# A DFT over 121 points folded in four 64x64 tiles, paired bn_stats, and two casts exchanged between VectorE and ScalarE

## The chip, the cores and the metric

The kernel runs on one core of a Trainium2 chip. The metric is the device time of one execution in microseconds (us). The engines are TensorE (PE, its weight loads shown as PEld), VectorE (DVE), ScalarE (ACT) and GpSimd (POOL); SyncE (SP) issues most DMAs. Each engine works through its own instructions in order and waits on semaphores for the others.

## The reference

The input is 64 images of 55 x 55 pixels with 96 channels. A depthwise convolution comes first, then one block of attention-like mixing by a Fourier transform over the 3025 pixels of each image, then a quantised feed-forward network (FFN).

```python
x = lat * x + bias + x                      # lat: depthwise convolution of x
t = x.reshape(64, 3025, 96)
n = layernorm(t)
h = relu(bn1(n @ w1.T))                     # 192 hidden channels
X = fft(h, axis=1, norm='ortho')            # over the 3025 tokens
xr = relu(X.real * rd - X.imag * idg + rb)
xi = relu(X.imag * rd + X.real * idg + ib)
y = ifft(xr + 1j * xi, axis=1, norm='ortho').real
t = t + bn2(y @ w2.T)
q = lambda v: float_quantize(v, 5, 2)       # fp8, 5 exponent bits
a = lambda v: float_quantize(v, 5, 10)      # fp16
u = relu(a(a(q(layernorm(t)) @ q(W1).T) + q(b1)))   # 384 hidden channels
t = t + a(a(q(u) @ q(W2).T) + q(b2))
```

Everything but the quantised FFN is in float32.

## The kernel before

The kernel has two stages. The first is the convolution over all images; its result goes to device memory (`t1s`). The second takes the 64 images one after the other as *sequences* of 3025 = 25 x 121 tokens, and the change lies wholly in it.

The transform of 3025 points is split into 121 x 25. Token n is written as 25 j + r, with j from 0 to 120 and r from 0 to 24. A tile `t` holds j on 121 partitions and r and the channels along the free dimension. The work of one sequence runs like this:

1. `load` fetches t. `stats` (L350) makes one `bn_stats` for each of the 25 values of r, 96 channels at a time, on DVE; the instruction returns count, mean and sum of squared deviations of the even and of the odd elements, six numbers. `variance` joins the two halves with small POOL instructions (L298 to L306, with the mean where it is needed later). `root` (ACT), `inverse` (DVE) and `newton` (POOL) make the reciprocal standard deviation.
2. In seven tiles i, of four values of r each (the last has one): `scale` (L363, POOL) makes xa; `turn` (L376, PE) transposes it into PSUM (pa); `turned` (L381, ACT) copies it to tnt, 96 channels and a row of ones on the partitions, 121 columns for each r.
3. For pairs of r: `hidden` (L397, PE) multiplies tnt with the 192 columns of w1e into ph, one matmul for each r, on 121 output partitions. `relu` (L406, ACT) makes h. `dft_j` (L412, PE) multiplies h with the constant f1, 121 rows by 128 columns: cosines and sines of the needed 61 frequencies, in a padded order. Since the input is real, only these are kept. `keep` (L416, ACT) copies the result pf to g. `put` (L432) sends g to a buffer `gd` in device memory with two DMAs, of 64 partitions each.
4. `fetch` (L451) reads it back with r on the partitions; `dft_r` (L478, PE, px) does the transform over r with 64x64 tiles; three ACT instructions (L495) and four DVE instructions (L504) apply the two relus of the frequency domain, POOL joins them (L511, sm and sr). `project` (L553, L563, PE, pd), `inverse_k1` (L583, pe) and their copies on ACT (L572, L592) go back, through device memory (`put_e`, L623), to `inverse_k2` (L644, py) and the `residual` (L655, DVE), which adds to t.
5. A second layer norm with `stats` (L661), `centre` (L677) and `quantise` (L686) on POOL, transposes (L695, pq) and their copies (L700). Then the FFN in nine pieces of 1008 or 1009 columns: `up` (L718, PE, pu), `cast` (L727) from PSUM to f16 on DVE (y16), `bias` with relu (L730) on DVE (z16), `quantised` (L742) from f16 to fp8 on ACT (hq); then `down` (L762, pw), a cast (L771, ACT), a bias (L776, DVE), the residual `add` (L782, POOL) and the `store` (L788).

Every such step is a *task* with an engine, an estimated cost, a list of tasks that it comes after, and the buffers that it makes and uses. `PLACES` gives each of a sequence's tasks a due place, in units of a sequence; tasks of up to five sequences are in flight. The function `ordered` walks through all 64 sequences with these costs before anything is issued, and the order that it finds is the order of instructions on each engine. It also knows the shape of the PE tiles (`edges`), and charges 0.09 for a change of shape (`SWITCH`). The first tasks of the first two sequences (`AHEAD`, `NAHEAD`) are issued under the convolution's end.

PSUM is held by two pools in this stage: `psn`, four buffers of 512 columns, for pa, ph, pf, pd, pe, py, pq and pw; and `psw`, two buffers of 1024 columns, for px and pu. A pool hands its buffers out in turn: the fifth request waits until the first buffer's last reader is done.

Of the kernel before, what the change touches and what calls it, by code (L numbers as in the profile page):

```python
# [11 lines left out]
F32 = mybir.dt.float32  # L12
# [34 lines left out]
NR1, NJ = 25, 121  # L47
KH, KHP = 31, 32
KC = 8
UPT = 1008  # L50

AHEAD, NAHEAD = 2, 10
# [5 lines left out]
    -0.85, -0.814, -0.754, -0.694, -0.634, -0.574, -0.232, -0.28, -0.28, -0.28, -0.26146, -0.13246,  # L58
    -0.13246, 0, 0, 0.074, 0.05, 0.06623, 0.06623, 0.14023, 0.11623, 0.15385, -0.129, 0, 0, 0.13246,
    0.13246, 0.20646, 0.18246, 0.19869, 0.19869, 0.27269, 0.24869, 0.30769, 0.00346, 0.13246, 0.13246,  # L60
    0.26492, 0.26492, 0.33892, 0.31492, 0.33115, 0.33115, 0.40515, 0.38115, 0.46154, 0.13592, 0.26492,
    0.26492, 0.39738, 0.39738, 0.47138, 0.44738, 0.46361, 0.46361, 0.53761, 0.51362, 0.61538, 0.26838,
    0.39738, 0.39738, 0.52985, 0.52985, 0.60385, 0.57985, 0.59608, 0.59608, 0.67008, 0.64608, 0.76923,
    0.40085, 0.52985, 0.52985, 0.66231, 0.66231, 0.73631, 0.71231, 0.72854, 0.72854, 0.80254, 0.77854,
    0.92308, 0.53331, 0.66231, 0.66231, 0.79477, 0.79477, 0.86877, 0.84477, 1.07692, 0.72, 0.97, 1.22, 1.47,
    0.9, 0.9, 0.9, 0.9, 0.9, 0.9, 0.9, 0.9, 0.774, 0.774, 1.046, 1.046, 1.046, 1.046, 1.046, 1.046, 1.046,
    1.046, 0.92, 0.92, 1.192, 1.192, 1.192, 1.192, 1.192, 1.192, 1.192, 1.192, 1.066, 1.066, 1.514, 1.534,
    1.534, 1.584, 1.584, 1.584, 1.66, 1.68, 1.68, 1.73, 1.73, 1.73, 1.73333, 1.338, 1.338, 1.338, 1.338,
    1.338, 1.338, 1.338, 1.338, 1.212, 1.212, 1.484, 1.484, 1.484, 1.484, 1.484, 1.484, 1.484, 1.484, 1.358,
    1.358, 1.63, 1.63, 1.63, 1.63, 1.63, 1.63, 1.63, 1.63, 1.504, 1.504, 1.952, 1.972, 1.972, 2.022, 2.022,  # L70
    2.022, 2.098, 2.118, 2.118, 2.168, 2.168, 2.168, 2.23333, 2.477, 2.677, 2.677, 2.687, 2.743, 2.743,
    2.753, 2.809, 2.809, 2.819, 2.875, 2.875, 2.885, 2.941, 2.941, 2.951, 2.975, 2.927, 2.927, 2.927, 2.835,
    2.835, 3.235, 3.235, 2.856, 2.856, 3.256, 3.256, 2.877, 2.877, 3.277, 3.277, 2.898, 2.898, 3.298, 3.298,
    2.919, 2.919, 3.319, 3.319, 2.94, 2.94, 3.34, 3.34, 2.961, 2.961, 3.361, 3.361, 3.509, 3.54, 3.509,
    3.509, 3.59436, 3.62536, 3.59436, 3.59436, 3.67972, 3.71072, 3.67972, 3.67972, 3.78836, 3.81936,
    3.78836, 3.78836, 3.87372, 3.90472, 3.87372, 3.87372, 3.95908, 3.99008, 3.95908, 3.95908, 4.06772,
    4.09872, 4.06772, 4.06772, 4.15308, 4.18408, 4.15308, 4.15308, 4.23844, 4.26944, 4.23844, 4.23844,
    3.466, 3.466, 3.466, 3.266, 3.516, 3.74536, 3.74536, 3.74536, 3.54536, 3.79536, 3.83848, 3.83848,
    3.83848, 3.63848, 3.88848, 4.02472, 4.02472, 4.02472, 3.82472, 4.07472, 4.10232, 4.10232, 4.10232,
    3.90232, 4.15232,  # L80
# [4 lines left out]
def conv_attn_hybrid(ctx, tc, a, out, t1s, tb, gds, eds):  # L85
# [48 lines left out]
    def ordered(bufs):  # L134
# [93 lines left out]
        t=5, sta=2, stc=1, xa=2, tnt=2, h=3, g=3, gd=2, gt=4, m=2, ar=2, nc=2, d1=2, sm=3, sr=2, d=4, e=2, ed=2,  # L228
        e2=1, xc=2, xq=2, tq=1, hq=1, y16=2, z16=2, o16=2, ot=3, rstda=2, rstdc=2, mean=2, psn=4, psw=2,
# [5 lines left out]
    def padding(pool):  # L235

        if pool == "tnt":
            of = ctx.enter_context(tc.tile_pool(name="p_tnt", bufs=1))  # L240
            padded[pool] = [of.tile([97, 4 * NJ], F32, tag=f"tnt{k}", name=f"tnt{k}") for k in range(2)]
            for x in padded[pool]:
                nc.gpsimd.memset(x[96:97, :], 1.0)
            return
        if pool == "hq":
            shape, dt, n, used = [128, 3, NJ * NR1 + 7], F8, 1, NJ * NR1
        else:
            shape, dt, n, used = [128, KC, 2, 64], F32, bufs[pool], 2 * NR1
        of = ctx.enter_context(tc.tile_pool(name=f"p_{pool}", bufs=1))
        padded[pool] = [of.tile(shape, dt, tag=f"{pool}{k}", name=f"{pool}{k}") for k in range(n)]  # L250
        for x in padded[pool]:
            v = x if pool == "hq" else x.rearrange("p k q n -> p (k q) n")
            nc.gpsimd.memset(v[:, :, used:], 0.0)
# [35 lines left out]
    def layernorm_tasks(b, what, t, after, mean):  # L289
# [5 lines left out]
        def variance():  # L295
            st_ = live[st]
            d, v = box["d"], box["v"] = small("d", name), small("v", name)
            nc.gpsimd.tensor_tensor(d, st_[:, :, 1], st_[:, :, 4], ALU.subtract)  # L298
            nc.gpsimd.tensor_tensor(v, st_[:, :, 2], st_[:, :, 5], ALU.add)
            nc.gpsimd.tensor_tensor(d, d, d, ALU.mult)  # L300
            nc.gpsimd.tensor_scalar(d, d, CH / 4.0, None, ALU.mult)
            nc.gpsimd.tensor_tensor(v, d, v, ALU.add)
            if mean is not None:
                m = make(mean, "mean", [NJ, NR1])
                nc.gpsimd.tensor_tensor(m, st_[:, :, 1], st_[:, :, 4], ALU.add)
                nc.gpsimd.tensor_scalar(m, m, 0.5, None, ALU.mult)  # L306

        def root():
            v, s = box["v"], small("s", name)
            box["s"] = s  # L310
            nc.scalar.activation(s, v, AF.Sqrt, bias=eps, scale=1.0 / CH)  # L311
            nc.scalar.activation(v, v, AF.Identity, bias=eps, scale=1.0 / CH)
# [11 lines left out]
        new = [(mean, "mean")] if mean is not None else []  # L324
        k = task("POOL", 1.9 if new else 1.45, variance, after, new=new, use=[st])
        k = task("ACT", 0.57, root, [k])
# [3 lines left out]
    def sequence(b):  # L330
# [13 lines left out]
        for q in range(5):  # L344

            def stats(q=q):
                if q == 0:
                    make(sta, "sta", [NJ, NR1, 6])
                for g in range(5 * q, 5 * q + 5):
                    nc.vector.bn_stats(live[sta][:, g, :], live[t][:, :, g, :])  # L350
# [3 lines left out]
            ks.append(task("DVE", 0.8, stats, after, new=new, use=[t] if new else [t, sta]))  # L354
        rstd = layernorm_tasks(b, "a", t, ks, None)
        g_done = []
        for i in range(7):
            g0, ng = 4 * i, min(4, NR1 - 4 * i)
            xa, pt, tnt = ("xa", b, i), ("pa", b, i), ("tnt", b, i)
# [20 lines left out]
            def turned(pt=pt, tnt=tnt, ng=ng):  # L380
                nc.scalar.copy(live[tnt][:CH, : ng * NJ], live[pt][:CH, : ng * NJ])  # L381
# [4 lines left out]
            turned_ = task("ACT", 0.1 + 0.087 * ng, turned, [k], use=[pt, tnt])  # L386
            ks = []
            for p in range(2 * i, min(2 * i + 2, 13)):
                nq = min(2, NR1 - 2 * p)
                ph, h, pf, g = ("ph", b, p), ("h", b, p), ("pf", b, p), ("g", b, i)  # L390

                def hidden(p=p, nq=nq, tnt=tnt, ph=ph, h=h):
                    x = make(ph, "psn", None)
                    make(h, "h", [NJ, 2 * H])
                    for q in range(nq):
                        g = 2 * (p % 2) + q
                        nc.tensor.matmul(  # L397
                            x[:NJ, q * H : (q + 1) * H],
                            live[tnt][:, g * NJ : (g + 1) * NJ],
                            w1e,  # L400
# [4 lines left out]
                def relu(nq=nq, ph=ph, h=h):  # L405
                    nc.scalar.activation(live[h][:, : nq * H], live[ph][:NJ, : nq * H], AF.Relu)  # L406

                def dft_j(p=p, nq=nq, h=h, pf=pf, g=g):
                    if p % 2 == 0:
                        make(g, "g", [4 * KHP, 4, H])  # L410
                    x = make(pf, "psn", None)
                    nc.tensor.matmul(x[:, : nq * H], f1, live[h][:, : nq * H], start=True, stop=True)  # L412

                def keep(p=p, nq=nq, pf=pf, g=g):
                    q0 = 2 * (p % 2)
                    nc.scalar.copy(  # L416
                        live[g][:, q0 : q0 + nq].rearrange("p q c -> p (q c)"), live[pf][:, : nq * H]
                    )

                k = task("PE", 0.326 * nq, hidden, [turned_], new=[(ph, "psn"), (h, "h")], use=[tnt])  # L420
                edges[k] = (FULL, FULL, 0.16, 0.16)
                k = task("ACT", 0.107 + 0.137 * nq, relu, [k], use=[ph, h])
                first = p % 2 == 0
                k = kj = task("PE", 0.325 * nq, dft_j, [k] + ([] if first else [kj]), new=[(pf, "psn")] + ([(g, "g")] if first else []), use=[h])
                edges[k] = (FULL, FULL, 0.16, 0.16 * nq)
                ks.append(
# [800 lines left out]
```

## Time and profile before

| | |
|---|---|
| median of three runs | 4573.0 us (4572.97 to 4574.33) |
| span of the profiled execution | 4570.5 us |
| convolution, filling and tail together | about 1048 us |
| one sequence, in the even part | 55.05 us |
| mean granted TensorE clock | 0.974 |

In the views of the profile, a line of a timeline has the start, the length (both in us), the engine, the line of the kernel, the operation, what it writes and reads, the shapes and how many are merged (xN); a float32 matmul appears as two records. A length is longer than the distance to the next instruction where the engine starts the next one before the first has ended; what an instruction costs its engine is the distance from start to start while work is waiting. A line of a stretch has its bounds, its length, and the busy time and number of instructions of PE, PEld, DVE, ACT and POOL, then the granted clock, the DMA share and GB/s. A line of the chain of waits has start, length and what held the end up.

### The profile page before, as it was taken

The numbers are of one execution on the slowest core, as the hardware profiler recorded it, in microseconds if no ns is written. First come the engines' busy times: TensorE is split into PE (matmuls) and PEld (weight loads), VectorE is DVE, ScalarE is ACT, GpSimd is POOL, SyncE is SP. The second block draws the span as 40 slices with busy tenths as digits, with TensorE's granted clock in tenths as the row PEclk, the third lists the DMA queues.
The fourth block names the chain that finished last, engine by engine and source line by source line (L and its number), as shares of the span: only waits on it lengthen the run. The fifth ranks groups of instructions, "written<-read, shape, count | busy, mean of one in ns | idle before, by whom it ended". The sixth has DMA issues, their size and how long they took to land.

```text
span 4570.5 us, 194901 instructions
## 1 busy us (share of the span) xinstructions
PE 4227.5 (92%) x83314; PEld 3487.6 (76%) x83314; DVE 3311.5 (72%) x7344; ACT 2953.9 (65%) x5947; POOL 3071.1 (67%) x4196
## 2 busy tenths in 40 slices
PE   8999898949999999999999999999999999999996
PEld 8989898937777777777777777777777777777774
DVE  5444344424788888888788788888888888888877
ACT  2000000017788888888888888888888888888875
POOL 2667676725666777777677676677777777667765
PEclk9999999969999999999999999999999999999996
DMA  4788888876666666766666666666666666667662
GB/s 178 180 206 207 247 197 196 198 171 168 167 176 177 177 180 179 186 179 178 178 181 182 177 175 179 177 180 179 177 182 181 184 182 177 179 175 181 178 173 79
DMA packets 572901, 823.11 MB, mean 180 GB/s; under 512 B 61641, under 2 KB 470924, under 8 KB 570754
## 3 DMA queue, kind: packets, MB, share of 16 engines
q1 hardware_dynamic: 449094, 741.40, 60.0%
q10 hardware_dynamic: 107996, 60.19, 7.0%
q0 software_dynamic: 14944, 9.06, 1.1%
q8 instruction: 655, 10.73, 1.0%
q14 instruction: 212, 1.74, 0.1%
HBM read 419.45 MB, written 390.64 MB: 177 GB/s over the span
## 4 chain that ended last, share of the span: by engine, by line
PE 62%; DVE 9%; DMA 9%; ACT 8%; issue 6%; POOL 4%; SPq 2%; ACTq 1%; POOLq 0%; DVEq 0%
PE pl L1000 13%; PE pf L412 9%; PE ph L397 8%; PE px L478 6%; PE pd L553 6%; PE py L644 4%; PE pu L718 3%; PE pd L563 3%; PE pe L583 3%; PE pa L376 2%; DMA x<-in_xc_dram 2%; PE pw L762 2%; DVE y L727 2%; POOL xq L686 1%; ACT m L495 1%
## 5 line engine op out<-in xcount | busy, mean ns | idle before, releaser
L1000 PE MATMUL pl<-x,toep 128*64 128x96 f32 (+1 forms) x18432 | 793.3, 250 | 75.4 <-DVE buf L1008 30.9
L1000 PEld LDWEIGHTS pl<-x,toep 128*64 128x64 f32 (+1 forms) x18432 | 785.8, 137 | 82.7 <-DVE buf L1008 32.0
L727 DVE CAST y<-pu 128x1008 f16<-128x1008 f32 (+1 forms) x576 | 688.6, 1201 | 197.7 <-PE pu L718 195.3
L397 PEld LDWEIGHTS ph<-w1e,tnt 97*121 97x121 f32 x3200 | 546.1, 185 | 247.5 <-issue 65.5
L397 PE MATMUL ph<-w1e,tnt 97*121 97x192 f32 x3200 | 670.1, 332 | 44.1 <-ACT g L416 26.4
L742 ACT ACTIVATE hq<-z 128x1008 fp8e5<-128x1008 f16 (+1 forms) x576 | 600.6, 1049 | 163.5 <-DVE z L730 162.9
L412 PE MATMUL pf<-h,f 121*128 121x384 f32 (+1 forms) x1664 | 667.9, 486 | 22.6 <-ACT h L406 16.0
L504 DVE SCALAR_TENSOR_TENSOR m<-px,par,m 128x400 f32<-128x400 f32 x768 | 480.7, 626 | 261.6 <-ACT ar L495 183.7
L311 ACT ACTIVATE sm_s_a<-sm_v_a,eps 121x25 f32<-121x25 f32 x64 | 20.4, 318 | 898.3 <-DMA t<-buf 876.3
L363 POOL TENSOR_TENSOR xa<-shared,rstda 121x384 f32<-121x384 f32 (+1 forms) x364 | 283.2, 781 | 366.7 <-PE pa L376 360.8
L478 PE MATMUL px<-m,gt 50*64 50x50 f32 x24576 | 453.0, 220 | 48.8 <-issue 42.9
L511 POOL TENSOR_TENSOR sm<-ar,m 128x400 f32<-128x400 f32 x256 | 269.9, 1054 | 339.0 <-DVE m L504 294.6
L478 PEld LDWEIGHTS px<-m,gt 50*64 50x64 f32 x24576 | 413.7, 135 | 107.7 <-issue 90.1
L1008 DVE SCALAR_TENSOR_TENSOR buf<-pl,x 121x384 f32<-121x384 f32 (+1 forms) x336 | 270.9, 842 | 291.8 <-PE pl L1000 176.9
L416 ACT COPY g<-pf 128x384 f32<-128x384 f32 (+1 forms) x832 | 385.8, 468 | 127.1 <-PE pf L412 62.7
L1018 POOL TENSOR_TENSOR buf<-buf,cbias 121x768 f32<-121x768 f32 (+1 forms) x168 | 303.4, 1819 | 237.2 <-DVE buf L1008 184.9
L553 PE MATMUL pd<-w2e,sm 128*64 128x96 f32 x8192 | 412.7, 252 | 33.3 <-ACT g L416 19.4
L406 ACT ACTIVATE h<-ph 121x384 f32<-121x384 f32 (+1 forms) x832 | 389.5, 488 | 66.5 <-PE ph L397 59.5
L730 DVE TENSOR_SCALAR z<-y,b1q 128x1008 f16<-128x1008 f16 (+1 forms) x576 | 418.2, 731 | 11.3
L553 PEld LDWEIGHTS pd<-w2e,sm 128*64 128x64 f32 x8192 | 354.5, 138 | 79.6 <-ACT g L416 23.9
L412 PEld LDWEIGHTS pf<-h,f 121*128 121x128 f32 x1664 | 293.3, 192 | 93.0 <-ACT h L406 24.0
L782 POOL TENSOR_TENSOR ot<-shared,o 121x480 f32<-121x480 f32 x260 | 304.3, 1178 | 81.2 <-DVE o L776 81.2
(129 smaller groups left out, 8639.3 us busy)
## 6 DMA issues: line engine op xcount, KB each, us to landing
gd<-g SPq DMA_DIRECT2D x768, 192.0 KB
gt<-gd SPq DMA_DIRECT2D x512, 288.0 KB
x<-in_xc_dram SPq DMA_DIRECT2D x240, 384.0 KB
out_dram<-ot SPq DMA_DIRECT2D x320, 210.0 KB
ed<-e SPq DMA_DIRECT2D x384, 150.0 KB
shared<-t SPq DMA_DIRECT2D x52, 1050.0 KB
t<-buf ACTq DMA_DIRECT2D x137, 288.0 KB
t<-shared ACTq DMA_DIRECT2D x65, 288.0 KB
```

The source lines that it names most:

```text
L397: nc.tensor.matmul(x[:NJ, q * H : (q + 1) * H], live[tnt][:, g * NJ : (g + 1) * NJ], w1e, start=True, stop=True,)
L406: nc.scalar.activation(live[h][:, : nq * H], live[ph][:NJ, : nq * H], AF.Relu)
L412: nc.tensor.matmul(x[:, : nq * H], f1, live[h][:, : nq * H], start=True, stop=True)
L416: nc.scalar.copy(live[g][:, q0 : q0 + nq].rearrange("p q c -> p (q c)"), live[pf][:, : nq * H])
L478: nc.tensor.matmul(x[to : to + 64].rearrange("p (q r n) -> p q r n", q=2, r=2)[:, k2p, :, o : o + NR1], y[rows, k % KC, c0 : c0 + 64], m1[ ...
L504: nc.vector.scalar_tensor_tensor(live[out_], view(px)[:, :, 256 : 256 + KC * NR1], scale, live[than], ALU.mult, ALU.max)
L553: nc.tensor.matmul(y[k % 2][64 * k2p : 64 * k2p + 64, k // 2 * CH : (k // 2 + 1) * CH], full[:, k, 64 * k2p : 64 * k2p + 64], w2e[:, 0, :] ...
L727: nc.vector.tensor_copy(live[y16][:, :n], live[pu][:, :n])
L730: nc.vector.tensor_scalar(make(z16, "z16", [128, 1024], F16)[:, :n], live[y16][:, :n], b1q[:, k : k + 1], 0.0, ALU.add, ALU.max,)
L742: nc.scalar.activation(live[hq][:, k, n0 : n0 + n], live[z16][:, :n], AF.Copy, saturate=False)
L782: nc.gpsimd.tensor_tensor(halves(y), live[t][:, :, 5 * q : 5 * q + 5], halves(live[o16]), ALU.add)
L1000: nc.tensor.matmul(pl[p : p + width, cc * NBS : (cc + 1) * NBS], toep[:, c0 + g + cc, o : o + width], xts[n, c0, m + d][:, g + cc, :], sta ...
```

## The change

- **The DFT over j is folded.** The rows j and 121 - j of h meet the same cosine and sines of opposite sign. So tnt now holds for each r two halves of 64 columns: j = 0 to 60 (61 columns, then padding), and the partners in reversed order (a column of zeros for j = 0, then j = 120 down to 61). `turned` needs two copies, the second with a negative stride. `hidden` runs twice a tile: side 1 gives the partners (phb), side 0 the front half (pha); each matmul has 64 output partitions, and two r go to the two halves of the partitions. One relu makes hb from phb; two DVE instructions (`fold`) make he = max(pha, 0) + hb and ho = max(pha, 0) - hb. `dft_j` is four matmuls of 64 rows by 64 columns a tile, into two PSUM buffers: cosines times he, sines times ho, for the even and the odd r.
- g and gd have another order, so that `put` is one DMA of 128 partitions instead of two of 64; the rows stay 768 bytes, and the fetch reads 6144 bytes in a row as before.
- **bn_stats is paired.** One instruction takes two values of r, interleaved, so that its even and odd halves are the two groups. 13 instructions replace 25 in each layer norm, and `variance` falls away: `root` reads the sum of squared deviations directly, and `centre` reads the mean from stc, which has two buffers now.
- **Two casts of the FFN are exchanged.** `cast` (pu to y16) goes from DVE to ACT, `quantised` (z16 to hq) from ACT to DVE.
- The list of places, the pools and the costs are fitted to the new tasks.

```diff
-AHEAD, NAHEAD = 2, 10
+AHEAD, NAHEAD = 2, 9
...
-        t=5, sta=2, stc=1, xa=2, tnt=2, h=3, g=3, gd=2, gt=4, ...
+        t=5, sta=2, stc=2, xa=2, tnt=2, hb=2, he=2, ho=2, g=3, gd=2, gt=4, ...
...
+    def pair_stats(st, t, i):
+        g0, ng = 2 * i, min(2, NR1 - 2 * i)
+        x = t[:, :, g0 : g0 + ng, :].rearrange("p h g c -> p h c g")
+        if ng == 1:
+            x = x.to_broadcast([NJ, 2, CHH, 2])
+        nc.vector.bn_stats(st[:, g0 : g0 + 2, :].rearrange("p g n -> p (g n)"), x)
...
-        k = task("POOL", 1.9 if new else 1.45, variance, after, new=new, use=[st])
-        k = task("ACT", 0.57, root, [k])
+        k = task("ACT", 0.45, root, after, use=[st])
...
             def turned(pt=pt, tnt=tnt, ng=ng):
-                nc.scalar.copy(live[tnt][:CH, : ng * NJ], live[pt][:CH, : ng * NJ])
+                p = live[pt][:CH, : ng * NJ].rearrange("p (g n) -> p g n", g=ng)
+                nc.scalar.copy(live[tnt][:CH, :ng, :MID], p[:, :, :MID])
+                nc.scalar.copy(live[tnt][:CH, :ng, 65 : 64 + MID], p[:, :, NJ - 1 : MID - 1 : -1])
...
+            def hidden(side, ...):
+                x = make(to[side], "psn", None)
+                at = slice(64 * side, 64 * side + 64)
+                for gg in range(ng):
+                    q, p = gg % 2, gg // 2
+                    nc.tensor.matmul(
+                        x[64 * q : 64 * q + 64, p * H : (p + 1) * H], live[tnt][:, gg, at], w1e, start=True, stop=True
+                    )
+            def relu(...):
+                nc.scalar.activation(live[hb][:nm, : np_ * H], live[phb][:nm, : np_ * H], AF.Relu)
+            def fold(to, op, ...):
+                nc.vector.scalar_tensor_tensor(
+                    live[to][:nm, : np_ * H], live[pha][:nm, : np_ * H], 0.0,
+                    live[hb][:nm, : np_ * H], ALU.max, op,
+                )
+            def dft_j(...):
+                for x, pf in enumerate(pfs):
+                    rows = slice(64 * x, 64 * x + 64)
+                    for y, h in enumerate((he, ho)):
+                        nc.tensor.matmul(
+                            live[pf][64 * y : 64 * y + 64, : np_ * H], f1[rows, y],
+                            live[h][rows, : np_ * H], start=True, stop=True,
+                        )
...
             def put(i=i, g=("g", b, i), g0=g0, ng=ng):
-                for k2p in range(2):
-                    nc.sync.dma_start(
-                        live[gd][k2p].rearrange("r q k c -> (q k) r c")[:, g0 : g0 + ng, :],
-                        live[g][2 * k2p * KHP : 2 * (k2p + 1) * KHP, :ng],
-                    )
+                nc.sync.dma_start(
+                    live[gd].rearrange("r q z k c -> (q z k) r c")[:, g0 : g0 + ng, :], live[g][:, :ng]
+                )
...
             def cast(pu=pu, y16=y16, n=n):
-                nc.vector.tensor_copy(live[y16][:, :n], live[pu][:, :n])
+                nc.scalar.copy(live[y16][:, :n], live[pu][:, :n])
...
-                nc.scalar.activation(
-                    live[hq][:, k, n0 : n0 + n], live[z16][:, :n], AF.Copy, saturate=False
-                )
+                nc.vector.tensor_copy(live[hq][:, k, n0 : n0 + n], live[z16][:, :n], saturate=False)
...
-    f1 = np.stack([c * kept, -s * kept], 2) / R
+    f1 = np.zeros((64, 2, 64))
+    f1[:MID] = np.stack([c * kept, -s * kept], 1)[:MID].reshape(MID, 2, 64) / R
```

## The prediction

> **What bounds the kernel now.** I read the page's totals first, then the busy time in stretches, then the chain of waits for the period of the loop, then the timelines of TensorE (PE) and VectorE (DVE).
>
> ```profile
> PE 4227.5 (92%) x83314; PEld 3487.6 (76%) x83314; DVE 3311.5 (72%) x7344; ACT 2953.9 (65%) x5947; POOL 3071.1 (67%) x4196
> ...
> 2000.00:3000.00 1000.00, 952.71 (x18227) 750.02 (x18227) 822.65 (x1898) 834.66 (x1682) 710.65 (x1059) 0.99 0.68 179
> ...
> 2520.92 0.71 PE pf L412 x2
> ...
> 2631.03 0.71 PE pf L412 x2
> ```
>
> The fourth line and the last are the same instruction two sequences later: 110.11 us, so 55.05 us a sequence. In the stretch from 2000 to 3000 us PE is recorded busy for 95%, ACT 83%, DVE 82%, POOL 71%. 64 x 55.05 = 3523 of the 4571 us span; the other 1048 us are the convolution, the start and the tail, which this change leaves alone.
>
> PE's 95% counts overlapping ends. What a matmul costs is the distance from start to start:
>
> ```profile
> 2507.88 0.81 PE L412 MATMUL pf<-h,f 121*128 121x384 f32 x2
> 2508.52 0.81 PE L397 MATMUL ph<-w1e,tnt 97*121 97x192 f32 x4
> 2509.17 0.27 PE L376 MATMUL pa<-ident,xa 121*96 121x121 f32 x1
> ...
> 2510.53 1.54 PE L553 MATMUL pd<-w2e,sm 128*64 128x96 f32 x32
> 2512.00 0.89 PE L563 MATMUL pd<-w2e,sr 64*64 64x96 f32 x32
> 2512.72 1.10 PE L478 MATMUL px<-m,gt 50*64 50x50 f32 x64
> ...
> 2531.52 0.81 PE L412 MATMUL pf<-h,f 121*128 121x384 f32 x2
> 2532.26 0.89 PE L583 MATMUL pe<-d,m 50*64 50x96 f32 x32
> 2533.08 0.62 PE L376 MATMUL pa<-ident,xa 121*96 121x121 f32 x4
> ```
>
> A full-array pass takes 0.84 ns a column: 0.65 us for the pf pair of 2 x 384 columns. Passes of 128x64 tiles run two at a time (32 passes of 96 columns in 1.47 us; one by one they would take 2.6), passes of 64x64 tiles four at a time (the same 32 in 0.72). Where the tile shape changes, pf to pe, the distance is 0.74 instead of 0.65, and the first four passes of the new shape are some 0.05 apart more: 0.14 us a change. Summed over a sequence (ph 8.1, pf 8.1, pa 2.6, px 5.8, pd 8.8, pe 2.8, py 4.0, pu 3.9, pw 3.2, pq 1.4, remaining changes of shape 1.2) PE needs about 49.9 us of the 55.05; it waits about 5.2, a share of 0.10. PE is the bound, with DVE's 45.3 (0.823 x 55.05) next to it.
>
> **PE's part.** The 25 row groups of a sequence go in six tiles of four and one of one. The DFT, L412, falls from 12 x 0.65 + 0.33 = 8.1 us to four 64x64 matmuls a tile, all four at once: 6 x 0.65 + 0.33 = 4.2. The hidden product has twice the matmuls with half the columns, two at a time, so 6 x 1.30 as before; the lone 25th group has no partner and costs 0.33 more. Counting neighbours in the built instruction order, changes of shape rise from 18.1 to 24.6 a sequence: 6.5 x 0.14 = 0.9. Sum: -3.9 + 0.3 + 0.9 = **-2.65 us** a sequence (bounds -3.9, every change hidden, and -1.4, twice that price for all added changes and for the lone group).
>
> One rule speaks against it. The Trainium skill, "TensorEngine Tiling (Array Packing)", section Key Properties, says that changing the tiling mode drains TensorE, and this case's 0.74 against 0.65 agrees. It gives no price, so by the rule the sum has no number.
>
> **DVE's part.**
>
> ```profile
> 2509.22 1.68 DVE L350 BATCH_NORM_STATS2 sta<-t 121x6 f32<-121x96 f32 x10
> 2510.82 1.18 DVE L727 CAST y<-pu 128x1008 f16<-128x1008 f32 x1
> 2512.05 0.48 DVE L730 TENSOR_SCALAR z<-y,b1q 128x1008 f16<-128x1008 f16 x1
> 2512.62 0.64 DVE L504 SCALAR_TENSOR_TENSOR m<-px,par,m 128x400 f32<-128x400 f32 x1
> 2513.18 0.63 DVE L504 SCALAR_TENSOR_TENSOR d<-px,par,nc 128x400 f32<-128x400 f32 x1
> ...
> 2608.09 1.09 DVE L730 TENSOR_SCALAR z<-y,b1q 128x1008 f16<-128x1008 f16 x1
> L940 DVE CAST w1q<-fw 96x384 fp8e5<-96x384 f32 x1 | 0.3, 342 | 0.0
> ```
>
> - Removed: nine casts y, start to start 1.11 to 1.21, taken as 1.16: -10.4.
> - bn_stats: 50 at 0.16 (ten in 1.60) are 8.0. Of 26 paired ones over 192 elements I have no row. From below 0.16; from above 0.43 (0.32 for two, and the stride that makes L1008's 384 elements cost 0.22 more than L504's 400, halved for 192). I take 0.27, 0.16 and 96 more elements at L504's slope: 7.0, so **-1.0** (-3.8 to +3.2).
> - Folds, new: 12 like L504 with 384 elements, 0.53, and two of 192 at 0.33: **+7.0**.
> - hq on DVE, new: f16 to fp8, 1008 elements. z is the same form with f16 out and takes 0.48 or 1.09; in the trace every z over 0.7 begins while a POOL instruction runs and ends 0.28 us after it, so it waits for POOL. The prologue's casts to fp8 (342 ns for 384 elements, 291 for 288) give 0.67 for 1008, start to start 0.59. Lower bound 0.40 (z undisturbed), upper 1.65 (0.59 behind a whole 1.06 us L511 instruction). hq stands directly behind its z, when a held POOL instruction is first in line, so I take more than z's mean excess of 0.3: 1.0 each, **+9.0** (3.6 to 14.9).
>
> The Trainium skill, "SBUF — State Buffer", section Who interferes with whom, states that a VectorE copy or cast in a two-port mode and a GpSimd instruction hold one port pair exclusively; z's waits agree. By it hq collides too, a cost above 0.59.
>
> DVE: 45.3 - 10.4 - 1.0 + 7.0 + 9.0 = 49.9 us a sequence. That no longer fits loosely under PE.
>
> **ACT, POOL, DMA.** ACT (0.835 x 55.05 = 46.0) changes hq (0.95) for y (0.36 for 384 columns at L416, so about 0.9 for 1008), drops 13 relus for 7 (-2.2) and cuts the copy of tnt in two (+0.1 to 0.25 each): about 44.5. pu's buffer in psw, which px shares, is then freed after 0.9 instead of 1.16. POOL loses both variance chains, twelve instructions near 0.25, -3.1 of 39.1; its L677 reads the mean with a stride now, which I leave at its 0.80. Both lie under PE's work; were the cover gone they would still be below it. The put's two DMAs a tile become one with the same 768 B rows, SP issues seven fewer a sequence, ahead of put_e and the stores in its queue. Larger zeroing of tnt and f1's new shape happen once, under the convolution's end, at nothing; without cover some 2 us.
>
> **The sum.** With PE's waits unchanged the period is 55.05 - 2.65 = 52.4. DVE then would be occupied 95%. If DVE, as a bound, waits the share that PE now waits, 0.10, the period is 49.9 / 0.90 = 55.4. Neither is the case: PE's waits grow, but PE has other work in line. I take the middle, **53.9**: 64 x 1.15 = 74 us. 4570.5 - 74 = 4497 for the span; the median of the runs, 4573.0, is 2.5 above the span: **4499 us**. DVE gives more than half of PE's saving back.
>
> **Rivals.**
> 1. *DVE's additions are hidden.* hq costs 0.59, folds fall in DVE's gaps (0.177 x 55.05 = 9.7 us idle now). Period 52.4: 4573 - 170 = 4403. For it: POOL has less to do, so fewer collisions. Against: DVE near 88% even then.
> 2. *The hidden product's PSUM buffer is held.* pha is freed only when both folds have run on DVE, where ph was freed by one relu on ACT. The pool psn has four buffers for nine kinds of product, and the fourth allocation after pha stops PE. DVE runs L504 in bursts of four (4 x 0.54 = 2.2 us), and a z with its hq may take 2. If PE stands 0.55 us for each of the seven tiles, 3.9 - 2.65 = +1.2 us a sequence: 4573 + 77 = **4650**. It decides from 2.65 / 7 = 0.38 us a tile. Against: by the built order, counted with the durations above, PE has 0.8 to 8.1 us of other work, median 4.3, between the product and its DFT.
> 3. *The four 64x64 matmuls don't run together* (they alternate over two moving tiles). Only two at once: the DFT stays at 8.1, PE at +1.2: 4650 too. L583 does the same with alternating tiles in 0.7 for 32, so I give it little.
>
> **Chances.** My case (4420 to 4555) 0.45, the first rival 0.15, the second 0.29, the third and other slowdowns 0.05, a balance within 0.2% of the time before, about what a measurement here can tell from no change, 0.06. Faster 0.60, same 0.06, slower 0.34. The range: below, the first rival with a tenth more of PE's saving, 4385; above, the second rival's 4650; outside lie strided bn_stats and colliding hq at their upper bounds together.
>
> **What would show it.** PE: pf start to start 0.65 for eight passes of 384; period 53 to 55. DVE: mean hq near 1.0, folds at 0.53, a busy share over 0.9 in the stretch from 2000 to 3000. Waits: PE behind DVE folds or for psn under 0.38 us a tile. I am wrong in the size if hq is near 0.6, and in the sign if pha's release stops PE.

## The result, and the profile after

The changed kernel takes 5156.4 us (median of four runs, 5131.0 to 5166.7) against 4573.7 beside it: a ratio of 1.126 with a 95% interval from 1.122 to 1.130. The change costs 583 us; the prediction had 4499 and a gain. The profiled execution has a span of 5157.1 us and a mean granted clock of 0.916 (0.974 before). With the same 1048 us outside the loop, a sequence takes (5157.1 - 1048) / 64 = 64.2 us instead of 55.05.

The totals of the page, and the stretch from 2000 to 3000 us (busy time of PE, PEld, DVE, ACT, POOL, then the granted clock), of the changed kernel:

```profile
PE 4435.9 (86%) x88178; PEld 3413.3 (66%) x88178; DVE 3481.1 (68%) x6704; ACT 2827.9 (55%) x6011; POOL 3014.3 (58%) x3432
...
2000.00:3000.00 1000.00, 857.77 (x16650) 618.40 (x16652) 742.35 (x1457) 679.50 (x1443) 591.62 (x716) 0.92 0.54 154
```

Every engine is less busy than before: PE 86% (95), DVE 74% (82), ACT 68% (83), POOL 59% (71). No engine is the bound; they wait for each other. The waits of PE and of DVE in that stretch (total, times, longest; about 15.5 sequences):

```profile
PE pe L604 <- DVE ho L407: 36.2, 26, 2.1
PE pw L781 <- DVE hq L763: 29.5, 15, 2.3
PE px L499 <- issue: 16.6, 14, 3.8
PE phb L399 <- ACT e L613: 14.3, 16, 1.0
PE pu L739 <- DVE nc L525: 10.4, 11, 1.2
```

```profile
DVE m L525 <- ACT ar L516: 132.9, 61, 5.1
DVE o L795 <- ACT o L790: 60.1, 62, 2.2
```

Before, the same two views began:

```profile
PE px L478 <- issue: 15.0, 16, 2.2
PE pd L553 <- ACT g L416: 6.5, 10, 0.8
```

```profile
DVE y L727 <- PE pu L718: 55.7, 57, 2.2
DVE m L504 <- ACT ar L495: 41.9, 31, 2.9
```

DVE now stands 133 us in 1000 with m at the head of its queue, waiting for ACT's ar, where it stood 42. What is queued behind m (folds, hq, nc) can come late, and PE stops for these: ho, hq and nc hold it up for 76 of the 142 us in 1000 that it is idle, where none of the longest waits of before was behind DVE. One such ring, from the timelines of PE, ACT and DVE:

```profile
2513.65 0.88 PE L604 MATMUL pe<-d,m 50*64 50x96 f32 x28 [2.09 <-DVE ho L407]
...
2518.33 0.48 PE L423 MATMUL pf<-he,f 64*64 64x384 f32 x1
...
2518.97 0.96 PE L499 MATMUL px<-m,gt 50*64 50x50 f32 x51
...
2521.39 0.87 PE L399 MATMUL phb<-w1e,tnt 97*64 97x192 f32 x8
...
2523.76 1.55 PE L399 MATMUL phb<-w1e,tnt 97*64 97x192 f32 x8 [0.86 <-ACT e L613]
...
2526.52 1.97 PE L499 MATMUL px<-m,gt 50*64 50x50 f32 x64
```

```profile
2514.43 0.86 ACT L613 COPY e<-pe 128x384 f32<-128x384 f32 x2 [2.14 <-PE pe L604]
...
2519.05 0.68 ACT L516 ACTIVATE ar<-px,par 128x400 f32<-128x400 f32 x1
```

```profile
2511.26 1.31 DVE L751 TENSOR_SCALAR z<-y,b1q 128x1009 f16<-128x1009 f16 x1
2512.50 0.55 DVE L407 SCALAR_TENSOR_TENSOR he<-pha,hb 128x384 f32<-128x384 f32 x1
2512.96 0.54 DVE L407 SCALAR_TENSOR_TENSOR ho<-pha,hb 128x384 f32<-128x384 f32 x1
2513.43 1.16 DVE L763 CAST hq<-z 128x1009 fp8e5<-128x1009 f16 x1
...
2519.77 0.63 DVE L525 SCALAR_TENSOR_TENSOR m<-px,par,m 128x400 f32<-128x400 f32 x1 [2.41 <-ACT ar L516]
```

PE stands 2.09 us at pe until DVE's ho has run, behind z. ACT stands 2.14 us for that pe; the px that ar reads comes behind pe on PE as well, so ar follows only at 2519.05, and DVE stands 2.41 us for ar. The wait goes round, and each queue keeps its written order. This is read from the order of the records; no run isolates one turn of the ring.

The last three lines of PE show a second cost. phb's eight passes take 0.87 us at 2521.39 and 1.55 at 2523.76; px's 64 take 1.97 where the timeline of before had 1.10. The granted clock of short stretches of the changed kernel:

```profile
2518.00:2519.00 1.00, 1.00 (x38) 0.66 (x32) 0.00 (x0) 1.00 (x3) 1.00 (x2) 1.00 0.16 37
2523.00:2526.40 3.40, 2.63 (x16) 1.72 (x16) 3.02 (x6) 1.98 (x5) 2.70 (x4) 0.50 0.99 222
```

At 2523 PE is granted 0.50. From 1200 us to 150 us before the end, the clock records of the changed kernel hold 628 us at half clock in 103 stretches; those of the kernel before 31 us in 8.

The 9.15 us a sequence can now be split. PE's idle share grows from 0.047 x 55.05 = 2.6 to 0.142 x 64.2 = 9.1 us: +6.5. PE is recorded busy for 594 of the 628 us. Taking work at half clock to last twice as long (0.87 and 1.55 us above), that is an estimated 594 / 2 over 3807 / 64.2 = 59.3 sequences, 5.0 us, against 0.3 before: +4.7. What remains of PE's busy time is 55.1 - 5.0 = 50.1 against 52.4 - 0.3 = 52.1: -2.0, where the prediction had -2.65 for PE's work. The saving is there, if a little smaller; stops and the clock take more than five times as much.

### The profile page after: what moved, and what is told of

It is laid out like the page before. It is cut to its first block, busy times and chain, and to the rows that moved or that the text cites. A ratio compares the mean times of both kernels' runs of the same rounds, so it can differ in the third digit from the quotient of the medians.

```text
span 5157.1 us, 203628 instructions
## 1 busy us (share of the span) xinstructions
PE 4435.9 (86%) x88178; PEld 3413.3 (66%) x88178; DVE 3481.1 (68%) x6704; ACT 2827.9 (55%) x6011; POOL 3014.3 (58%) x3432
## 5 line engine op out<-in xcount | busy, mean ns | idle before, releaser
L1019 PE MATMUL pl<-x,toep 128*57 128x96 f32 (+1 forms) x18432 | 793.4, 250 | 72.6 <-issue 30.3
L1019 PEld LDWEIGHTS pl<-x,toep 128*57 128x57 f32 (+1 forms) x18432 | 785.1, 137 | 80.8 <-issue 35.9
L748 ACT CAST y<-pu 128x1008 f16<-128x1008 f32 (+1 forms) x576 | 575.7, 1013 | 237.4 <-PE pu L739 225.1
L763 DVE CAST hq<-z 128x1008 fp8e5<-128x1008 f16 (+1 forms) x576 | 547.4, 959 | 9.9 <-DVE z L751 0.5
L499 PE MATMUL px<-m,gt 50*64 50x50 f32 x24576 | 500.7, 228 | 59.6 <-issue 55.1
L399 PE MATMUL phb<-w1e,tnt 97*64 97x192 f32 x3200 | 395.9, 357 | 108.1 <-ACT g L432 52.3
L423 PE MATMUL pf<-he,f 64*64 64x384 f32 (+1 forms) x1664 | 444.2, 494 | 49.8 <-DVE he L407 30.7
L317 POOL TENSOR_TENSOR sm_s_c<-rstdc 121x25 f32<-121x25 f32 x64 | 65.8, 1029 | 599.4 <-DVE rstdc L313 599.4
L739 PE MATMUL pu<-tq,w1q 96*128 96x512 fp8e5 (+2 forms) x1152 | 374.3, 416 | 48.0 <-DVE nc L525 35.6
L423 PE MATMUL pf<-ho,f 64*64 64x384 f32 (+1 forms) x1664 | 400.6, 496 | 6.1 <-issue 3.5
L593 ACT COPY d<-pd 128x384 f32<-128x384 f32 x512 | 221.4, 486 | 336.3 <-PE pd L584 336.2
```

The lines of the kernel that those rows point to most:

```text
L399: nc.tensor.matmul(x[64 * q : 64 * q + 64, p * H : (p + 1) * H], live[tnt][:, gg, at], w1e, start=True, stop=True)
L423: nc.tensor.matmul(live[pf][64 * y : 64 * y + 64, : np_ * H], f1[rows, y], live[h][rows, : np_ * H], start=True, stop=True,)
L499: nc.tensor.matmul(x[to : to + 64].rearrange("p (q r n) -> p q r n", q=2, r=2)[:, k2p, :, o : o + NR1], y[rows, k % KC, c0 : c0 + 64], m1[ ...
L739: nc.tensor.matmul(p[:, c0:c1], w1q[:, k * 128 : (k + 1) * 128], live[tq][:, n0 + c0 : n0 + c1], start=True, stop=True,)
L748: nc.scalar.copy(live[y16][:, :n], live[pu][:, :n])
L763: nc.vector.tensor_copy(live[hq][:, k, n0 : n0 + n], live[z16][:, :n], saturate=False)
```

## The experiments

Two theories are tested. **Order**: the list of places was made for other tasks (276 of the 290 places of the changed kernel are values of the old list), the order that follows from it lets engines wait for each other, and any part that is blamed is only where the wait shows. **Parts**: one edit costs the time, through late hq on DVE, through pha's PSUM buffer held behind the folds (the second rival of the prediction; "the hold" below), or through the pairs. The first two runs set late hq against the hold; the order comes in with the two after them. Times are to be read beside 5156 and 4573.

### One part alone, or undone

The changed kernel with the casts back on their engines, in instructions and costs:

```diff
-                nc.scalar.copy(live[y16][:, :n], live[pu][:, :n])
+                nc.vector.tensor_copy(live[y16][:, :n], live[pu][:, :n])
...
-                nc.vector.tensor_copy(live[hq][:, k, n0 : n0 + n], live[z16][:, :n], saturate=False)
+                nc.scalar.activation(live[hq][:, k, n0 : n0 + n], live[z16][:, :n], AF.Copy, saturate=False)
```

> The changed kernel with the two casts put back (y on DVE, hq on ACT); fold and paired bn_stats stay. Late hq (hq on DVE, behind z and behind POOL, makes PE wait 2.05 us at pw, and what follows from that wait is the loss): 4600 or less. The hold (folds keep pha's PSUM buffer, PE stops 2.1 us at pe): 5000 or more, because the folds and DVE's load are as before the undoing (removing hq at 0.92 and adding y at 1.16 gives DVE +2 us a sequence).

Measured 5079.0, ratio 1.108 (1.093 to 1.124). PE no longer waits for hq, yet only 77 us come back out of 583. Late hq alone doesn't explain the loss. The number is where the theory of the hold put it, but the costs changed with the casts, so this run has a new order too and doesn't show the hold.

The kernel before with the opposite edit, the exchange alone:

> The kernel before with the exchange of the casts alone. DVE falls by 9 x (1.16 - 0.92) = 2.2 us a sequence, ACT stays. Late hq: 4750 or more, PE waiting at pw for DVE. The hold: 4520 to 4620, no loss without the folds.

Measured 4826.3, ratio 1.053 (1.047 to 1.060). That is where late hq was expected, though PE's stops behind hq are only 15.0 us in 1000. This run has a new order as well; the control below shows what that can be worth.

The kernel before with `pair_stats` in place of `bn_stats` and `variance`, and nothing else:

> The kernel before with paired bn_stats alone. DVE -1.1 us, POOL -3.1 us a sequence. Both theories: 4500 to 4590, little change, since neither engine was the bound. A third one, that reading the statistics with a stride or the missing POOL step disturbs the order: above 4650.

Measured 4745.3, ratio 1.035 (1.031 to 1.040): slower by 164 us, though DVE and POOL have less to do and no instruction of PE changed. Both theories had expected little change. Each of the two parts tried alone costs something, whatever it relieves. That speaks for something that they share, and each of these kernels drew a new order. The fold alone was not tried.

The changed kernel with costs that its own profile shows:

```diff
-            x = task("DVE", 0.4, bias, [x], new=[(z16, "z16")], use=[y16])
+            x = task("DVE", 0.69, bias, [x], new=[(z16, "z16")], use=[y16])
...
-            hq_done[s, k] = task("DVE", 0.62, quantised, ...)
+            hq_done[s, k] = task("DVE", 0.92, quantised, ...)
...
-            k = task("DVE", 0.6, bias, [k], use=[o16])
+            k = task("DVE", 0.72, bias, [k], use=[o16])
```

> The changed kernel, planned with the durations that its trace shows (hq 0.92 instead of 0.62, z 0.69 instead of 0.40, the FFN's second bias 0.72 instead of 0.60); the instructions are the same, their order is another. Wrong order (the plan takes DVE for faster than it is, so that PE meets waits it was not to meet): 4700 or less. The hold as a matter of buffers, whatever the order: 5000 or more.

Measured 4955.0, ratio 1.081 (1.077 to 1.086): 201 us less with every instruction the same. It lies between the two expectations: another order helps, but these costs alone don't bring a good one.

### The order alone

The control: the kernel before, with one constant of its planner changed by 0.006.

```diff
-    FULL, SWITCH, NEAR, RING = "128x128", 0.09, 0.359, 8
+    FULL, SWITCH, NEAR, RING = "128x128", 0.09, 0.365, 8
```

> The kernel before, with one constant of the planner changed: NEAR, the reach within which a later task may be taken first, 0.365 instead of 0.359. Every instruction is the same, only the order differs. If the order alone costs as much as the change's single parts did (pairs 1.035, casts 1.053 with lighter engines): 4750 or more. If the parts themselves were the cause: 4560 to 4600.

Measured 4866.5, ratio 1.063 (1.060 to 1.067). The same instructions in another order cost 289 us, half of what the change costs. DVE's wait for ar is 104 us in 1000 here too, and 218 us pass at half clock. The 164 and 245 us of the two single parts lie within what an order alone can do, so they say nothing of pairs or casts.

The same on the changed kernel, NEAR at 0.268 and at 0.256:

> The changed kernel with one constant of the planner changed, NEAR from 0.359 to 0.268; every instruction, cost and place is as it was, only the order that the planner draws differs. Its own period falls from 58.3 to 54.2. Theory of the order: 4750 to 4950, a saving of more than 200 with nothing of the work changed. If the changed work itself costs the time: within 60 of 5156.

> The same with NEAR at 0.256; the planner's period is 56.6, between. Theory of the order: 4850 to 5150, and at any rate another time than the changed kernel's by more than 60. If the changed work itself costs the time: within 60 of 5156.

Measured 4862.1 (1.060 to 1.067 of before) and 4942.8 (1.079 to 1.086), both as the theory of the order expected. The changed kernel's instructions take 5156, 4943 or 4862 us as the planner's own period (what a sequence takes when the planner plays the loop through with its costs) goes from 58.3 over 56.6 to 54.2. The stretch of the run with 0.268:

```profile
2000.00:3000.00 1000.00, 913.33 (x17955) 638.08 (x17957) 760.25 (x1568) 728.40 (x1556) 625.47 (x773) 0.97 0.59 165
```

PE is busy 91% and its clock is 0.97; DVE's wait for ar has fallen to 53 us in 1000. PE's stops behind ho are no longer among its waits and those behind hq are down to 4.0, although the folds hold pha's buffer as before.

### The same order, one dependence or engine changed

These runs leave the planner's input alone, so that the order is that of the changed kernel. First, folds that never read pha:

```diff
                 nc.vector.scalar_tensor_tensor(
                     live[to][:nm, : np_ * H],
-                    live[pha][:nm, : np_ * H],
+                    live[hb][:nm, : np_ * H],
                     0.0,
                     live[hb][:nm, : np_ * H],
```

> The changed kernel with its order of instructions and all costs as they are; the two folds of a tile read hb twice (max(hb, 0) + hb and max(hb, 0) - hb) in place of pha and hb, so the PSUM buffer of pha has no reader and is free as soon as it is written. The output is therefore not the reference's: the front half of the hidden product is left out of the folds. All instructions stay. Theory of the hold (rival 2 of the prediction): PE's stops behind ho (36 us in 1000) vanish, with them about 2.3 us a sequence, 150 us, and at least as much again from the clock that halves behind these stops: 4850 or less. Theory of the order (the order written for all engines doesn't fit, the hold is only one place where that shows): other stops take their place, 5000 to 5130.

Measured 5354.9, ratio 1.170 (1.165 to 1.174). PE's stops of pe behind ho are gone, as the theory of the hold said, but the time rose by 200, outside both expectations. The groups of DVE show a confound (something else that differs too), the fold of the changed kernel first, then that of this run:

```profile
L407 DVE SCALAR_TENSOR_TENSOR ho<-pha,hb 128x384 f32<-128x384 f32 x94 | 51.3, 546 | 0.0
```

```profile
L407 DVE SCALAR_TENSOR_TENSOR ho<-hb 128x384 f32<-128x384 f32 x87 | 80.6, 927 | 0.0
```

With both operands in SBUF the same 384 columns take 0.93 us on average instead of 0.55. The mean hides two kinds. The folds of this run that meet no POOL instruction take 0.55; those that run beside one take 1.09 (he) and 1.27 (ho) on average, and the long ones end 0.41 us after the POOL instruction during which they began. In the changed kernel the folds beside POOL take 0.55 like the others. So the next two runs shortened the folds, once with pha as in the diff and once with hb in its place:

```diff
-                    live[to][:nm, : np_ * H],
-                    live[pha][:nm, : np_ * H],
+                    live[to][:nm, :H],
+                    live[pha][:nm, :H],
...
-                            live[h][rows, : np_ * H],
+                            live[h][rows, None, :H].to_broadcast([64, np_, H]),
```

> The changed kernel with its order as it is; each fold does only the first 192 of its 384 columns, and the DFT matmuls read these columns twice, so PE's work is the same. The output is not the reference's: the second pair of r of each tile is left out. This is the control of the next run: folds of about 0.35 instead of 0.55 us, pha still read and so still held. If the length of the folds on DVE decides: some 5 us a sequence less on DVE, up to 300 us off 5156. If the order decides: 4950 to 5150.

> As the control run beside it (folds of 192 columns), but the folds read hb twice and never pha, so that pha's PSUM buffer is free as soon as PE has written it. In the earlier run without the hold PE's stops behind ho vanished, but each fold of 384 columns took 0.92 instead of 0.55 us; of 192 columns it should take 0.35 to 0.55, no more than the folds of the changed kernel. Theory of the hold: 150 us or more below the control. Theory of the order: within 80 of the control, with PE stopped at other places.

Measured 5119.1 (1.116 to 1.121) with pha, 5325.2 (1.161 to 1.167) without. The first says that 2 x 0.2 us less on DVE in each tile is worth 37 us in all: the length of the folds isn't the cause. The second, outside both expectations, is still confounded: its folds take 0.72 on average against 0.35. At last folds of 64 columns, read six times by the DFT:

> As the earlier runs without the hold (folds read hb twice, never pha; order kept), with folds of 64 columns, which the DFT matmuls read six times; the output is not the reference's. With 384 and 192 columns these folds took 0.92 and 0.72 us, 0.2 less for 192 columns fewer; 64 columns should take about 0.55, what the changed kernel's folds take, so that nothing but the hold differs from it. Theory of the hold: 150 us or more below 5156, that is at most 5000. Theory of the order: the stops behind ho go, others come, 5060 to 5260.

Measured 5133.2, ratio 1.120 (1.116 to 1.124). The folds take 0.62 us on average (0.55 in the changed kernel), but again in two kinds, as the POOL lines and the folds beside them show:

```profile
2515.22 1.03 POOL L532 TENSOR_TENSOR sm<-ar,m 128x400 f32<-128x400 f32 x1 [1.34 <-DVE m L525]
2516.21 1.04 POOL L532 TENSOR_TENSOR sm<-d,nc 128x400 f32<-128x400 f32 x1
```

```profile
2515.54 0.80 DVE L407 SCALAR_TENSOR_TENSOR he<-hb 128x64 f32<-128x64 f32 x1
2516.26 1.07 DVE L407 SCALAR_TENSOR_TENSOR ho<-hb 128x64 f32<-128x64 f32 x1
2517.26 0.21 DVE L407 SCALAR_TENSOR_TENSOR he<-hb 128x64 f32<-128x64 f32 x1
2517.39 0.21 DVE L407 SCALAR_TENSOR_TENSOR ho<-hb 128x64 f32<-128x64 f32 x1
```

So the mean is nearly matched, but the delays are not: some folds are far shorter than 0.55 us and others far longer. PE's longest waits:

```profile
PE pw L781 <- DVE hq L763: 72.7, 30, 2.7
PE pf L423 <- DVE he L407: 10.5, 12, 1.0
```

The 36.2 us behind ho are zero, the 29.5 behind hq have become 72.7, and the time differs by 23 us, with intervals that overlap. That is what the theory of the order expected: with the hold gone, PE stops at the next thing that DVE has late. But in all three runs without the hold the stops behind hq are 73 to 85 us, against 31 in the run with short folds that keeps it, and the folds that wait for POOL may bring part of that. The price of the hold alone is therefore not shown by these runs. What speaks against it as the cause is the redrawn order above (4862) and the fitted one below (4765), where pha is held as before and the stops behind ho are gone or small.

The casts on their former engines, at the places that the changed order gives them (the first diff above, without the costs):

> The changed kernel with its order as it is, but the two casts of the FFN issued on their former engines at the places that they have now: y on VectorE, hq on ScalarE. The earlier run that undid the exchange also drew a new order; this one does not. If the exchange itself (hq late on VectorE, 30 us of PE's stops in 1000) is the cause: below 4950. If the order is the cause: within 100 of 5156, either way.

Measured 5512.6, ratio 1.204 (1.200 to 1.208). Neither theory had that number: the order theory allowed 100 us either way. An order written for y on ACT is worse by 356 us with y on DVE, where it now stands before folds and m. The sign still speaks against the exchange as the cause, but the run says as much about an order that fits neither kernel.

### Places fitted anew

For these kernels the list of places and NEAR were sought anew by random steps that shorten the planner's own period; z, o, and hq where it is on DVE, had the costs shown above. First the changed kernel and, in the same way, the kernel before:

> The changed kernel with the same instructions, but another order: places and NEAR fitted to the new tasks with the measured durations of z, hq and the second bias. The order as the cause: 4700 or less, the granted clock over 0.95, PE's waits at pe and pw gone. The hold of pha as a matter of four buffers: 5000 or more, PE still behind ho.

> The kernel before with the same fitting of places and NEAR and the measured durations of z and the second bias; the same instructions. If the order of before was already as good as this fitting makes it: 4500 to 4620. If a better order is to be had for before as well, below 4500, and a gain of e6 is no gain of the change.

Measured 4765.1 (1.037 to 1.045) and 4600.5 (1.003 to 1.008). The changed kernel gets 391 of its 583 us back with no instruction changed; the kernel before gains nothing, its own places were as good. The theory of the order had expected more, 4700 or less and a clock over 0.95; the clock is 0.933. In the fitted kernel neither pe behind ho nor pw behind hq is among PE's large waits; the largest is now

```profile
PE pa L356 <- POOL xa L343: 28.9, 26, 1.6
```

Some 165 us are left between the two. In the two profiled runs (spans of 4760.0 and 4572.1 us, 2.9 us a sequence apart) the changed kernel has 421 us at half clock against 55. By the estimate used above that is 3.0 us a sequence more, the size of what is left; PE's idle time is 2.5 us more and its remaining work 2.5 us less. For the 165 us, a second fit of the changed kernel and fits of the parts:

> The changed kernel's instructions with places fitted a second time, from another random start, to the same measured costs; the planner's own period is 53.7 against 53.3 of the first fit, which took 4765. If what is left over the kernel before (165 us over the kernel before fitted in the same way) lies in the work itself: 4730 to 4830 again. If it is the luck of one order: anywhere from 4570 to 4950, and likely more than 50 from 4765.

> The kernel before with paired bn_stats alone, as in the earlier run that took 4745, but with the places fitted anew to its tasks, with z at 0.69 and o at 0.72 in the planner. Theory of the order: the pairs cost nothing in themselves and relieve DVE by 1 to 2 and POOL by 3 us a sequence; fitted, 4540 to 4610, that is at or below the 4600 that the kernel before took when its own places were fitted in the same way. Rival, the pairs cost something themselves (a strided read, a chain that is longer, buffers of stc): above 4660.

> Fold and pairs without the exchange of casts, places fitted anew (planner's period 54.4 against 53.3 for the whole change). If the fold's longer chain (two products, relu, two folds on DVE, four matmuls) is what the fitted change has left over the kernel before: 4750 to 4900, not below the whole change's 4765. If the exchange of the casts is: below 4700.

> The kernel before with its DFT as it was, with paired bn_stats and the exchange of casts, places fitted anew (planner's period 51.4, the lowest of all; 52.65 for the kernel before). If the fold alone costs what is left, and the other two parts help once the order fits: 4500 to 4620. If the exchange costs too (hq on VectorE beside POOL): 4650 to 4800.

| with places fitted | us | ratio, 95% |
|---|---|---|
| kernel before | 4600.5 | 1.003 to 1.008 |
| + pairs | 4629.3 | 1.008 to 1.015 |
| + pairs + casts | 4688.1 | 1.021 to 1.028 |
| + pairs + fold | 4714.8 | 1.027 to 1.035 |
| + all three | 4765.1 | 1.037 to 1.045 |
| + all three, second fit | 4823.1 | 1.049 to 1.060 |

Two fits of one kernel lie 58 us apart, so a step of 30 or 60 in this table is no measurement of a part. By the expectations, 4714.8 fits neither blame (fold 4750 or more, casts below 4700), and 4688.1 is where a price of the casts was expected. Pairs alone were 164 us slower with unfitted places and are 29 slower than the fitted kernel before. That falls between the two expectations, nearer the order's. The kernels with the fold come out highest, though 4715 against 4688 is within that scatter, and none beats the kernel before as it stands. Whether more fitting would close the last 165 us, or whether the fold's longer chain and the casts keep them, stays open. Between kernels the planner's period doesn't rank the times either: 51.4 for pairs and casts (4688), 52.65 for the kernel before.

## Why the prediction was wrong

**The sizes held.** The profile of after shows, against the prediction's terms:

- *PE.* Four 64x64 tiles do run together: the eight passes of 384 columns that begin at 2518.33 are followed by px at 2518.97, 0.64 us later (predicted 0.65). PE's work fell by an estimated 2.0 a sequence by the split above (-2.65 predicted, bounds -3.9 and -1.4). The third rival is excluded.
- *DVE.* Its busy time is 0.742 x 64.2 = 47.7 us a sequence (49.9 predicted). Folds follow each other after 0.46 us (2512.50, 2512.96; 0.53 predicted). hq takes 0.91 for 1008 columns and 1.10 for 1009 by its groups (1.0 predicted, start to start); of those with 1008 columns, 0.66 when it begins beside no POOL instruction and 1.40 behind one, as the prediction argued. Seven paired bn_stats at 2532.73 take 1.85 us to the next instruction, 0.264 each (0.27 predicted). That estimate, made between 0.16 and 0.43 with no row for it, was right.
- *ACT and POOL.* 0.680 x 64.2 = 43.6 (44.5 predicted), 0.592 x 64.2 = 38.0 (36.0 predicted, low by 2).

**The step that failed** is in the sum: "With PE's waits unchanged the period is 55.05 - 2.65 = 52.4 ... If DVE, as a bound, waits the share that PE now waits, 0.10, the period is 49.9 / 0.90 = 55.4 ... I take the middle, 53.9". It took the waits of 5.2 us a sequence as belonging to the kernel, to be shared out by load. They belonged to one order. The change altered the set of tasks, their engines and places, so the planner wrote a new order for all engines. In it PE's idle time and half clock grew by an estimated 11.2 us a sequence, more than three times the whole range between the two ends of that step. The control shows about half of the measured 9.15 us with no change of work at all: 289 us, 4.5 us a sequence, from a step of 0.006 in one constant. No sum of loads can see that; the built order, which the prediction read only for changes of shape and for PE's work between product and DFT, was not followed for DVE, where m waits for ar.

One number that was at hand before any run pointed the right way. The planner plays the whole loop through with its costs, and its own period was 52.65 us for the kernel before and 58.3 for the changed one: 5.6 us a sequence, 360 us in all. Computed in the same way, the control has 57.7 us. The prediction took the order from this planner and did not read its period. It is a warning and not a time, as the kernels that it ranks wrongly show.

**The first rival** (DVE's additions hidden, 4403) is as wrong as the forecast, by the same step. **The second rival** named the place: PE does stop for pha's buffer, 36.2 us in 1000, that is 36.2 x 64.2 / 1000 = 2.3 us a sequence or 0.33 a tile, just under its point of 0.38. But freeing the buffer gave 23 us, in a run whose folds wait for POOL, so its price of 0.55 us a tile is neither confirmed nor cleanly refuted; in the redrawn and the fitted order the stops go without freeing it. The argument used against this rival, that PE has a median of 4.3 us of other work between product and DFT, failed because that work, here pe, needs a buffer of psn too and stops until ho has run.

**The clock** was absent from the prediction. It may be half of the loss: 4.7 of 9.15 us by the estimate above. It wasn't isolated by a run, but over the runs it grows with the time: 31 us at half clock in the kernel before, 55 in its fitted form (4600), 218 at 4866, 421 at 4765, 423 at 4943, 628 at 5156, 1007 at 5513. The order of these isn't strict, so the clock is not the whole of it.

## What to carry to other kernels

In a kernel whose order is written ahead for all engines, an edit to any task is also a new order, and here that cost more (289 us) than either part that was tried alone (164 and 245): draw the order once more with nothing else changed, as a control, before a time is put down to an edit. If the planner has a period of its own, compare it first. When all engines grow less busy and the time rises, read the waits of the engines that are *not* the bound as well; the longest of them (DVE for ar, 133 us in 1000) pointed to the ring, where PE's own waits pointed to its symptoms. To test one edit, hold the order and change the instruction, and look at the single durations as well as at their mean: folds of 0.21 and of about 1 us had a mean of 0.62 here. To judge an edit's worth, fit the order again, twice, and compare it with a fit of the old kernel.

## What the runs showed of the hardware

- The granted clock of TensorE goes to 0.50 for about 3.41 us or multiples of it (6.8 and 10.2 also occur). In the ring shown it fell at 2523.0, after stops of 2.09 and 1.08 us and at the start of one of 0.86, not at once behind the first. Over the 103 stretches at half clock of the changed kernel, PE stood still for 54% of the 3.41 us before the clock fell, on average, and for 14% of all the time. The Trainium skill, "TensorE: Matmul & The Clock Gate", Part 1: The HAM clock gate, gives two clock states, half and full, and a window of 3.4 us, which agrees. It puts the half clock after at least one idle window; in the kernel before no stop in the loop was longer than 2.6 us, and the clock still fell eight times, so here the measurement decides.
- A DVE instruction with two operands in SBUF waits for a running POOL instruction, and the same one with an operand in PSUM does not. With both in SBUF, 384, 192 and 64 columns take 0.55, 0.35 and 0.21 us beside no POOL instruction; those that wait end 0.41, 0.21 and 0.08 us after the POOL instruction during which they began, and the means are 0.93, 0.72 and 0.62. With an operand in PSUM, 384 and 192 columns take 0.55 and 0.345 beside POOL or not. The Trainium skill, "SBUF — State Buffer", section Who interferes with whom, says that an instruction with two inputs in SBUF contends with a GpSimd instruction that reads SBUF, and that one with at most one such input does not, outside the two-port modes; the runs agree. Moving an operand out of PSUM to free a buffer can thus cost more than the buffer.
- A paired bn_stats of 192 elements, read with a stride, takes 0.264 us start to start, and two of 96 took 0.32.
